# A decoder layer with a quantised feed-forward network: one more pair of blocks by two levels, and left sums built by accumulating loads

## The chip, the cores and the metric

The kernel runs on one core of one Trainium2 chip, in float32. The metric is device microseconds of one execution (us), the median of several runs. The engines are TensorE (PE, matmuls; its weight loads are listed as PEld), VectorE (DVE), ScalarE (ACT), GpSimd (POOL) and SyncE (SP, which only issues DMAs). DMAs are issued from a queue in order; those issued by SyncE and ScalarE are listed as hardware queues, those by GpSimd as a software queue. Loads that add to what their destination holds ("accumulating loads") are issued by GpSimd here.

## The reference

`x` is (16, 128, 1024), the context the same. Three residual parts follow one another; the last is most of the work:

```python
x = x + attention(layernorm(x), Wqkv, bqkv, Wo, bo)
x = x + linear_cross_attention(layernorm(x), context, ...)
x = x + ffn(layernorm(x), gate, up, down)

def dequantize(W_q, scale, zero):        # two 4-bit numbers to a byte
    w = stack([W_q >> 4 & 15, W_q & 15], -1).reshape(out, -1, 64)
    return ((w - zero[:, :, None]) * scale[:, :, None]).reshape(out, 2 * half)

g = einsum('bsh,ih->bsi', x, Wg)         # 1024 -> 2752
u = einsum('bsh,ih->bsi', x, Wu)
return einsum('bsi,hi->bsh', silu(g) * u, Wd)   # 2752 -> 1024
```

## The kernel before

The attention and the cross attention run first (until 756 us of the span). The feed-forward network is computed with Winograd's form of Strassen's scheme: a product of two 2x2 block matrices takes seven block products in place of eight, and sums of blocks on both sides and of the results.

**Gate and up.** The 2752 inner columns are cut into eleven blocks (`BLOCKS`): ten full ones of 256 columns and a remainder, `RB`. The tokens are cut into two passes (`PASSES`). A full block goes either by one level (`one_block`: seven products for gate and seven for up, matmuls of 128x512) or, two blocks at a time, by two levels (`two_levels`: seven outer products `DOWN` = 1, 2, 6, 5, 3, 7, 4, each of seven inner ones, matmuls of 128x256). A one-level block is 112 matmuls of 512 columns, a pair by two levels 196 of 256; each shows as two records in the trace's chain. In the first pass blocks 0 to 3 go by one level (block 0 beside the end of the cross attention), then the pairs in `PAIRS = [2, 3, 4]` by two levels, then `last_block` for the remainder; in the second pass all five pairs go by two levels, then the remainder. The inner left sums (`inner_left`, tiles li) are made by GpSimd, the inner right ones (ti) and the sums of the results (`got`, tiles U, V, C) by DVE; ACT copies banks (k) and applies silu. `finish` makes the products h of a quarter of a block (two halves of the tokens, two parities of the inner columns) and `store` puts them out to `h_all[blk, q, half]` in DRAM. DVE, GpSimd, ACT and SyncE follow an order written out by hand here (`InOrder`); `soon_due` and `extra` are lists of DVE steps that `multiply`'s neighbours take up one by one.

**What h is stored for.** Down takes h as the left matrix of an outer Strassen step as well: parity of the inner columns by pass. The first pass stores h as parts 1 and 2, the second as part 4 and, by `combine_h`, four combinations: 7, 5, 6 and 3. For these `load_first` loads parts 1 and 2 again (tiles hl), and DVE makes four subtractions and additions of 128x512 (tiles hc) a block and half. For the remainder `last_combinations` does the same at the start of down.

**Preparation of the weights.** `prepare` is a generator, and each `next` of it is one step. For each block and matrix it loads packed bytes (`raw`) and scales and zeros (`sz`; for down `szd`), turns them to float32 on DVE (tiles pa), makes the sums for the scheme (pc) and stores all to `wprep` in DRAM. Down's matrix ("d") takes two units a block, one for each half s; the unit with s = 1 makes one sum besides. The list `todo` is cut in three: twelve jobs in the attention (`early`), six in the cross attention (`middle`), the others in the first pass (`rest`), among which stand down's eleven blocks. `rest` is advanced by `beside` at fixed products of one-level blocks and by the last argument of `two_levels`, once an outer product.

**Down.** Seven outer steps `DOWN`, for each of which `operands` loads 20 blocks of h (tiles lq, 256 KB each, SyncE) and 10 of weights (wq), with `remainder` for the remainder's (lr, 96 rows; wr). Weights whose sum isn't stored are loaded with `load_sums`: the first term by SyncE, the next by GpSimd as an accumulating load on the same tile. `TERMS` says which: steps 5, 6 and 4 have two terms. For step 6 the sum is stored again (`kept_sums`), as step 4 uses it. Each step has seven inner products (`INNER` = 1, 5, 6, 7, 3, 4, 2), with inner sums lc and wc by DVE (`combine`), one step ahead of their use. The order of instructions in down is chosen by a scheduler. While TensorE runs step n, the loads of step n + 1 are issued. After inner product 6, DVE adds the bank to what it kept (iu, iv); then TensorE's small `extra` product for the remainder takes the same bank 6 (`po6`).

**Attention.** `early` is advanced at fixed places of the loop over four groups of tokens t: one or two steps at each f of t > 0, and (3, 3, 4, 2) steps after each `attend`. The cross attention's first load of the context (cxt) is issued after the attention.

Of the kernel before, what the change touches and what calls it, by code (L numbers as in the profile page):

```python
# [44 lines left out]
TERMS = {1: "0", 2: "2", 3: "3", 5: "01", 6: "40", 7: "4", 4: "52"}  # L45
# [13 lines left out]
class Route:  # L59


    def __init__(self, engine):
        self.engine = engine
# [17 lines left out]
def decoder_layer(  # L81
# [137 lines left out]
    def prepare(jobs, ahead, queue, vector=nc.vector, sync=nc.sync, loads_first=False):  # L219
# [4 lines left out]
        stores = deque()  # L224
        if loads_first:
            yield
# [5 lines left out]
        for k, (blk, mat, s) in enumerate(units):  # L232
# [4 lines left out]
            put()  # L237
            raw, scale, zero = loads.popleft()
            if k + ahead < len(units):
                loads.append(load_raw(*units[k + ahead], sync))  # L240
# [13 lines left out]
            if mat == "d":  # L254

                for n in range(2):
                    terms = [pair[:, n].bitcast(I32), zero[:, n]]
                    if n != s:
                        terms.reverse()
                    vector.tensor_tensor(pair[:, n], *terms, ALU.subtract)  # L260
                vector.tensor_tensor(pair, pair, scale, ALU.mult)
                if s == 0:
                    out = wprep[blk, mat] = dram.tile([6, *size], F32, name=f"wd{blk}", tag=f"wd{blk}")
                for n in range(2):
                    stores.append((wprep[blk, mat][QUARTERS.index((n, s))], pair[:, n]))
                if s == 1:
                    t = pools["c"].tile([P, 512], F32, name="pc")[: size[0]]
                    vector.tensor_tensor(t, pair[:, 0], pair[:, 1], ALU.add)
                    stores.append((wprep[blk, mat][4], t))
                yield  # L270
                continue
            pair = pair.rearrange("p n (j f) -> p (n j) f", f=P)
            vector.tensor_tensor(pair, pair.bitcast(I32), zero, ALU.subtract)
            vector.tensor_tensor(pair, pair, scale, ALU.mult)
# [15 lines left out]
            def comb(a, b, op):  # L290
                t = pools["c"].tile([P, 512], F32, name="pc")[: size[0]]
                vector.tensor_tensor(t, a, b, op)
                return t
# [17 lines left out]
    down = deque((blk, "d") for blk in range(len(BLOCKS)))  # L311
    for n in range(len(todo) - 1, MIDDLE, -1):
        todo[n:n] = [down.popleft() for _ in range(2)]
    todo += down
# [25 lines left out]
    with (  # L340
# [166 lines left out]
        for t in range(NT):  # L507
# [14 lines left out]
            for f in range(4):  # L522
# [9 lines left out]
                if t > 0:  # L532
                    for _ in range(1 + f % 2):
# [21 lines left out]
            for _ in range((3, 3, 4, 2)[t]):  # L555
                next(early, None)
# [480 lines left out]
    def operands(oq):  # L1037

        lb, wb = {}, {}
        for kc, half in ((0, 1), (0, 0), (1, 1), (1, 0)):  # L1040
            for i in range(NI):
                t = lb[kc, half, i] = pools["lq"].tile([P, TB], F32, name="lq")
                nc.sync.dma_start(t, h_all[2 * i + kc, oq, half])
# [4 lines left out]
    def load_right(oq, kc, wb):  # L1048
        for i in range(NI):
            wb[kc, i] = pools[f"wq{kc}"].tile([P, 512], F32, name="wq")  # L1050
        load_sums(oq, [(wb[kc, i], wprep[2 * i + kc, "d"]) for i in range(NI)])

    kept_sums = []

    def load_sums(oq, tiles):


        for n, term in enumerate(TERMS[oq]):
            for t, quarters in tiles:
                src = quarters[int(term)]  # L1060
                if n == 0:
                    nc.sync.dma_start(t, src)
                else:
                    nc.gpsimd.dma_start(t, src, accum_op=ALU.add)  # L1064
                    if oq == 6:
                        kept_sums.append((quarters[5], t))
# [15 lines left out]
    with ExitStack() as gs:  # L1082
# [38 lines left out]
        PAIRS = [2, 3, 4]  # L1121
# [40 lines left out]
        def combine_h(blk, half, h00, h10, h01, h11, engine, delay=2):  # L1162

            w = BLOCKS[blk][1]
            made = {}

            def comb(q, a, b, op):
                t = made[q] = chc.tile([P, TB], F32, name="hc", tag="hc")[:w]
                engine.tensor_tensor(t, a, b, op)
                store(blk, q, half, t, delay)  # L1170

            return [
                lambda: comb(7, h00, h01, ALU.subtract),
                lambda: comb(5, h01, h11, ALU.add),
                lambda: comb(6, made[5], h00, ALU.subtract),
                lambda: comb(3, h10, made[6], ALU.subtract),
            ]
# [82 lines left out]
        def last_block(ps, T, between):  # L1260


            keys = {0: (1, 2), 1: ("e", 4)}[ps]
# [7 lines left out]
            def small(half, x, u):  # L1271
# [5 lines left out]
                def mult():  # L1277
                    rows = ds(REST, REST)
                    t = ch.tile([P, TB], F32, name="h", tag="h")
                    vector.tensor_tensor(t[rows], u[rows], g[rows], ALU.mult)  # L1280
# [39 lines left out]
            def got(k, ps, add):  # L1320
# [4 lines left out]
                elif k == (1, 0):  # L1325
                    t = ch.tile([P, TB], F32, name="h", tag="h")
                    vector.tensor_tensor(t, ps, add, ALU.add)
                    vector.tensor_tensor(t, t, done[half], ALU.mult)
                    finish(half, t)
                else:  # L1330
                    t = done[half] = ct.tile([P, TB], F32, name="sg", tag="sg")
                    if add is None:
                        nc.scalar.activation(t, ps, AF.Silu)
                        vector.tensor_tensor(t, up[half], t, ALU.mult)
# [83 lines left out]
        def inner_left(L, pool, tag):  # L1418
# [9 lines left out]
            def comb(k):  # L1428
                t = L[k] = pool.tile([P, 2, CHUNKS, P], F32, name="li", tag=tag, bufs=8 if tag == "hc" else 4)
# [10 lines left out]
        def two_levels(ps, pairs, operands, between=lambda i, q: None):  # L1440
# [77 lines left out]
            def finish(i, q):  # L1518
# [5 lines left out]
                def mult(f):  # L1524
                    t = ch.tile([P, 2, HT], F32, name="h", tag="h")
                    pair = C[:, ts(f, 2)]
                    vector.tensor_tensor(t, pair[:, :, 1], pair[:, :, 0], ALU.mult)
# [3 lines left out]
                    elif s == 1:  # L1531
                        store(2 * i + f, 4, half, t)
# [3 lines left out]
            def combine(i, half, hl):  # L1536
                steps = [
                    combine_h(
                        2 * i + f,
                        half,  # L1540
                        hl[:, f, 0],
                        hl[:, f, 1],
                        hs[0, half, f],
                        hs[1, half, f],
                        vector,
                        delay=1,
                    )
                    for f in range(2)
                ]

                extra.extend(steps[f][k] for part in (0, 2) for f in range(2) for k in (part, part + 1))
# [12 lines left out]
            for n, (i, q) in enumerate(OUTERS):  # L1564
                last = n + 1 == len(OUTERS)
                if q in (1, 5):
                    sums["U" if q == 1 else "V"] = place.tile(
                        wide, F32, name="U" if q == 1 else "V"
                    )
# [19 lines left out]
                if ps == 1 and n == 0:  # L1589
                    extra.append(last_operand)  # L1590
                multiply(n, 2)
# [26 lines left out]
                between(i, q)  # L1618


                if ps == 0:
                    pass
                elif q == 3:
                    while extra:
                        extra.popleft()()
                    hl = load_first(i, 1)
                elif q == 7:
                    soon_due.append(lambda i=i, hl=hl: combine(i, 1, hl))
                elif q == 1 and i > 0 or last:
                    while soon_due:  # L1630
                        soon_due.popleft()()
                    do_extra(0, len(extra))
                    hl = load_first(i if last else i - 1, 0)
                    combine(i if last else i - 1, 0, hl)
# [4 lines left out]

        def load_first(i, half):  # L1640

            hl = xres.tile([P, 2, 2, TB], F32, name="hl", tag="X6")
            for f in range(2):
                for k in (1, 2):
                    tc.keep_in_program_order(
                        nc.sync.dma_start(hl[:, f, k - 1], h_all[2 * i + f, k, half])
                    )
            return hl
# [10 lines left out]
        def beside(n, mat, q):  # L1659
# [6 lines left out]
            if blk == 2 * PAIRS[0] - 1:  # L1666
                if n == 7:
                    route.engine = nc.sync
                    right.extend(first_operands.inner_right(DOWN[0]))
# [16 lines left out]
            elif blk == 2 * PAIRS[0] - 1:  # L1686
                steps = n in (0, 1, 2, 4, 12)
            elif blk == 1 and mat == "g":
                steps = n in (4, 5)
            else:  # L1690
                steps = n % 7 < 5 and (blk == 1 or n not in (3, 10))
# [4 lines left out]
        for blk in order:  # L1696
            if blk is None:
                two_levels(
# [3 lines left out]
                    lambda i, q: (q == 6 or i > PAIRS[0] and q not in (3, 7)) and next(rest, None),  # L1702
                )
                deep.close()
# [6 lines left out]
            if blk == 2 * PAIRS[0] - 1:  # L1711
                first_operands.pool = deep.enter_context(
                    tc.tile_pool(name="c_d", bufs=1, reuse_waits="tile")
                )
# [7 lines left out]
        chc = pool("c_hc", 8)  # L1722
# [3 lines left out]
        remaining = two_levels(1, range(NI), second_operands)  # L1726
# [16 lines left out]
    with ExitStack() as dst:  # L1743
# [7 lines left out]
        dh = pool("d_h", 4)  # L1751
# [6 lines left out]
        def last_combinations(half):  # L1758

            h = {}  # L1760
            for q in (4, "e", 1, 2):
                h[q] = dh.tile([P, TB], F32, name="dh")[:RW]
                nc.sync.dma_start(h[q], h_all[RB, q, half])
            for q, dst, a, b, op in (
                (5, 4, "e", 4, ALU.add),
                (7, "e", 1, "e", ALU.subtract),
                (6, 1, 4, 1, ALU.subtract),
                (3, 2, 2, 1, ALU.subtract),
            ):
                nc.vector.tensor_tensor(h[dst], h[a], h[b], op)  # L1770
                new_h(RB, q, half)
                nc.scalar.dma_start(h_all[RB, q, half], h[dst])

        def remainder(oq):
# [236 lines left out]
```

## Time and profile before

| | us |
|---|---|
| median of 3 runs (2205.85 to 2206.42) | 2206.3 |
| the profiled execution | 2204.94 |
| its span, first to last instruction | 2203.1 |
| TensorE busy | 2176.4 (99%) |
| DVE busy | 1522.8 (69%) |
| ACT busy | 515.7 (23%) |
| GpSimd busy | 722.3 (33%) |
| DMA, mean over the span | 210 GB/s |

TensorE's clock is granted in full throughout. The span in stages: attention to 253, cross attention to 756, block 0 beside its end, blocks 1 to 3 of the first pass from 820.65, its three pairs from 964.85, its remainder from 1224.7, the second pass's five pairs from 1262.5, its remainder from 1685.5, down from 1723.3 in seven steps of 67.4 us. Busy time is a share of engine time and says nothing of what waits for what. For that the chain of waits is read, which follows the work that ended last back to what released each step, and the idle time of TensorE with its releaser.

### The profile page before, as it was taken

Reading aid. Unit: us, or ns where it says so; the run is one execution under the profiler, and the core shown is the slowest. Engines: PE = TensorE matmul, PEld = TensorE weight load, DVE = VectorE, ACT = ScalarE, POOL = GpSimd, SP = SyncE. Lnnn points to the kernel's source line nnn. Section 1 sums busy time; section 2 is a strip of 40 time slices with the busy share of each in tenths; the row PEclk is TensorE's granted clock in tenths of the full one; section 3 lists DMA queues with packets and bytes.
Section 4 is the critical chain, followed back from the end, with each engine's and each line's share of the span. In section 5 each row is a group of like instructions: output and inputs, shape, how many; then the busy total and the mean of one; then the engine's idle time right before and its main releaser. Section 6 shows DMA issues by size and latency. Waiting matters only on the chain.

```text
span 2203.1 us, 24889 instructions
## 1 busy us (share of the span) xinstructions
PE 2176.4 (99%) x8668; PEld 1582.2 (72%) x8668; DVE 1522.8 (69%) x2077; ACT 515.7 (23%) x698; POOL 722.3 (33%) x686
## 2 busy tenths in 40 slices
PE   8999999999999999999999999999999999999998
PEld 7566555555555554468888588888887788888887
DVE  6897677888887776748788677667666635554472
ACT  2111135655665541112121112112211000000000
POOL 5453124333343364624444234444441011000100
PEclk9999999999999999999999999999999999999999
DMA  6436447768797698967777736566565988534931
GB/s 255 160 129 195 161 136 233 230 221 243 231 292 219 190 296 274 319 212 248 249 246 262 218 132 217 172 206 211 174 226 198 324 238 258 156 115 140 264 121 40
DMA packets 262102, 463.43 MB, mean 210 GB/s; under 512 B 28096, under 2 KB 121024, under 8 KB 257872
## 3 DMA queue, kind: packets, MB, share of 16 engines
q1 hardware_dynamic: 216304, 361.06, 51.0%
q0 software_dynamic: 27360, 81.55, 11.8%
q10 hardware_dynamic: 18304, 19.14, 2.8%
q8 instruction: 71, 1.16, 0.2%
q14 instruction: 63, 0.52, 0.1%
HBM read 297.14 MB, written 163.97 MB: 209 GB/s over the span
## 4 chain that ended last, share of the span: by engine, by line
PE 92%; DVE 5%; issue 1%; DMA 1%; ACT 0%; POOL 0%; SPq 0%; DVEq 0%; ACTq 0%; POOLq 0%
PE q L77 27%; PE po L1888 21%; PE p L77 10%; PE kq L77 10%; PE mm L77 8%; PE kx L77 5%; PE mm L422 4%; PE p L1210 2%; DVE pa L77 2%; PE mm L437 2%; PE mm L320 1%; DVE C L77 1%; PE tr L369 1%; DVE h L77 0%; DVE ti L77 0%
## 5 line engine op out<-in xcount | busy, mean ns | idle before, releaser
L77 PE MATMUL q<-ti,li 128*128 128x256 f32 x1344 | 308.9, 380 | 0.7 <-ACT k L77 0.6
L77 PEld LDWEIGHTS q<-ti,li 128*128 128x128 f32 x1344 | 255.5, 190 | 36.0 <-POOL li L77 1.0
L77 ACT COPY k<-q 128x512 f32<-128x512 f32 x168 | 98.3, 585 | 532.6 <-PE q L77 532.5
L852 POOL TENSOR_TENSOR qe<-qe,qrec 128x1024 f32<-128x1024 f32 x64 | 148.3, 2317 | 179.6 <-DVE qrec L77 142.2
L77 POOL TENSOR_TENSOR li<-w 128x512 f32<-128x512 f32 x112 | 154.3, 1379 | 119.5 <-PE q L77 64.4
L1888 PE MATMUL po<-wc,lc 128*128 128x256 f32 x840 | 183.4, 379 | 0.0
L1888 PEld LDWEIGHTS po<-wc,lc 128*128 128x128 f32 x840 | 159.9, 190 | 21.5
L77 POOL TENSOR_TENSOR li<-w,li 128x512 f32<-128x512 f32 x56 | 73.2, 1308 | 210.5 <-PE q L77 200.6
L77 PE MATMUL p<-b,w 128*128 128x512 f32 x304 | 133.9, 593 | 0.0
L77 DVE TENSOR_TENSOR C<-q,k 128x512 f32<-128x512 f32 x120 | 82.3, 685 | 70.8 <-PE q L77 66.8
L77 PE MATMUL kx<-ek,cxt 128*128 128x512 f32 x256 | 123.7, 606 | 4.6 <-DMA cxt<-in_cxt 4.6
L1888 PE MATMUL po<-wq,lq 128*128 128x256 f32 x560 | 126.7, 379 | 0.2 <-issue 0.2
L77 PEld LDWEIGHTS mm<-qs,m_sb 128*128 128x128 f32 x512 | 97.4, 190 | 39.7 <-issue 29.1
L77 DVE STREAM_TRANSPOSE kt<-qe 128x1024 f32<-128x1024 f32 x64 | 79.3, 1240 | 62.0 <-POOL qe L852 57.8
L77 PE MATMUL q<-b,w 128*128 128x256 f32 x512 | 121.0, 380 | 0.0
L77 PE MATMUL mm<-qs,m_sb 128*128 128x256 f32 x512 | 120.8, 380 | 0.0
L77 PE MATMUL kq<-wq_sb,xn 128*128 128x512 f32 x256 | 120.2, 593 | 0.4 <-ACT qe L840 0.4
L77 PE MATMUL kq<-wk_sb,cx 128*128 128x512 f32 x256 | 120.6, 594 | 0.0
L1888 PEld LDWEIGHTS po<-wq,lq 128*128 128x128 f32 x560 | 106.2, 190 | 15.6 <-issue 1.1
L77 DVE TENSOR_TENSOR pa<-pa,sz 128x1024 f32<-128x1024 int32 x86 | 112.7, 1311 | 2.4
L1064 POOL DMA_DIRECT2D wr<-wd x3 | 2.6, 854 | 336.7 <-DMA lq<-h 180.5
L422 PE MATMUL mm<-xnT,wqkv_sb 128*128 128x512 f32 (+1 forms) x320 | 112.5, 508 | 0.2 <-DVE xnT L77 0.2
(214 smaller groups left out, 3929.2 us busy)
## 6 DMA issues: line engine op xcount, KB each, us to landing
w<-wu SPq DMA_DIRECT2D x140, 256.0 KB, 3.4
lq<-h SPq DMA_DIRECT2D x140, 256.0 KB, 4.5
w<-wg SPq DMA_DIRECT2D x138, 256.0 KB, 2.8
kd<-kt SPq DMA_DIRECT2D x62, 512.0 KB, 3.6
qs<-kd SPq DMA_DIRECT2D x244, 128.0 KB, 3.2
ti<-r SPq DMA_DIRECT2D x22, 1024.0 KB, 7.3
h<-hc SPq DMA_DIRECT2D x80, 256.0 KB, 3.0
wq<-wd SPq DMA_DIRECT2D x70, 256.0 KB, 6.0
```

What stands on the lines that cost most here:

```text
L77: return lambda *args, **kw: self._tc.keep_in_program_order(fn(*args, **kw))
L320: tensor.matmul(ps, oT[:, d, ts(b % BPT, S)], wo_d[d][:, ts(h, 512)], start=(d == 0), stop=(d == 1),)
L369: nc.tensor.transpose(tr[:, j, :], xn[:, ts(4 * h + j, P)], ident)
L422: nc.tensor.matmul(ps[:, tokens], wqkv_sb[:, f, c, :], xnT[:, c, tokens], start=(c == 0), stop=(c == CC - 1),)
L437: nc.tensor.matmul(ps, xnT[:, c, ts(i, S)], wqkv_sb[:, 4:6, c, :], start=(c == 0), stop=(c == CC - 1),)
L852: nc.gpsimd.tensor_tensor(qe, qe, rec.unsqueeze(2).to_broadcast(wide), ALU.mult)
L1064: nc.gpsimd.dma_start(t, src, accum_op=ALU.add)
L1210: tensor.matmul(ps, wt[:, j, :], T[q][:, :, j], start=(first == q and j == 0), stop=(q in (2, 3, 4) and j == JC - 1), skip_group_check=True,)
L1888: nc.tensor.matmul(bank[:, i, :], l[:, ts(i, S)], w,  start=(start and c == 0 and i % 2 == 0), stop=(stop and c == len(pairs) - 1), skip_g ...
```

## The change

1. `PAIRS` becomes `[1, 2, 3, 4]`: blocks 2 and 3 go by two levels in the first pass.
2. Of down's weights only blocks 0 to 3 (`LATE`) are prepared in the first pass. The other seven (14 units) are prepared beside the second pass's pairs by a second generator, `downs`, whose loads have one buffer each. `two_levels` takes the generator and a function that says how many of its steps to put into `extra` at each outer product; with `fine`, a step is cut in two.
3. Each block of down's weights has its sum for step 6 stored too (t6), so that step 6 loads one term, without an accumulating load.
4. The second pass makes its products with the sign turned (`product`), stores them as parts "e" and 4, and makes one sum, part 5 (`add_up`). `combine_h`, `load_first` and `last_combinations` go.
5. In down the left operands come by `load_sums` too: `H_TERMS` says from which parts, `REST_TERMS` the same for the remainder. The second term of steps 6, 3 and 7 is an accumulating load by GpSimd, 20 blocks in each, and the remainder's have one or two (steps 6, 5, 3, 7). Step 6's left sums are stored again as part 6, which step 3 reads. Signs in down's `got` follow.
6. In the attention, two early steps are taken up sooner: at t = 2 two at each f, and none after the last `attend`.

```diff
-TERMS = {1: "0", 2: "2", 3: "3", 5: "01", 6: "40", 7: "4", 4: "52"}
+TERMS = {1: (0,), 2: (2,), 3: (3,), 5: (0, 1), 6: (5,), 7: (4,), 4: (5, 2)}
+H_TERMS = {1: (1,), 2: (2,), 6: (5, 1), 5: (5,), 3: (2, 6), 7: (1, "e"), 4: (4,)}
+REST_TERMS = {**H_TERMS, 6: ("e", 4, 1), 5: ("e", 4)}
...
+            if ahead == 0:
+                loads.append(load_raw(*units[k], sync))
+                yield
             raw, scale, zero = loads.popleft()
...
+                if fine.fine:
+                    yield
                 vector.tensor_tensor(pair, pair, scale, ALU.mult)
...
                 if s == 1:
-                    t = pools["c"].tile([P, 512], F32, name="pc")[: size[0]]
-                    vector.tensor_tensor(t, pair[:, 0], pair[:, 1], ALU.add)
-                    stores.append((wprep[blk, mat][4], t))
+                    t7, t6 = (pools["c"].tile([P, 512], F32, name="pc", tag="hc", bufs=4)[: size[0]] for _ in range(2))
+                    vector.tensor_tensor(t7, pair[:, 0], pair[:, 1], ALU.add)
+                    stores.append((out[4], t7))
+                    vector.tensor_tensor(t6, t7, A[0, 0], ALU.add)
+                    stores.append((out[5], t6))
...
-    down = deque((blk, "d") for blk in range(len(BLOCKS)))
-    for n in range(len(todo) - 1, MIDDLE, -1):
-        todo[n:n] = [down.popleft() for _ in range(2)]
-    todo += down
+    LATE = 4
+    todo += [(blk, "d") for blk in range(LATE)]
...
-                    for _ in range(1 + f % 2):
+                    for _ in range(2 if t == 2 else 1 + f % 2):
                         next(early, None)
...
-            for _ in range((3, 3, 4, 2)[t]):
+            for _ in range((3, 3, 4, 0)[t]):
...
             for i in range(NI):
-                t = lb[kc, half, i] = pools["lq"].tile([P, TB], F32, name="lq")
-                nc.sync.dma_start(t, h_all[2 * i + kc, oq, half])
+                lb[kc, half, i] = pools["lq"].tile([P, TB], F32, name="lq")
+            load_sums(
+                H_TERMS[oq],
+                [(lb[kc, half, i], h_parts(2 * i + kc, half)) for i in range(NI)],
+                oq if oq == 6 else None,
+                kept_last if (kc, half) == (1, 0) else kept_sums,
+            )
...
+    def load_sums(terms, tiles, keep=None, kept=None):
+        for n, term in enumerate(terms):
+            for t, parts in tiles:
                 if n == 0:
-                    nc.sync.dma_start(t, src)
+                    nc.sync.dma_start(t, parts[term])
                 else:
-                    nc.gpsimd.dma_start(t, src, accum_op=ALU.add)
-                    if oq == 6:
-                        kept_sums.append((quarters[5], t))
+                    nc.gpsimd.dma_start(t, parts[term], accum_op=ALU.add)
+                if keep is not None and n == len(terms) - 1:
+                    kept.append((parts[keep], t))
+
+    def keep_sums(kept):
+        while kept:
+            nc.gpsimd.dma_start(*kept.pop(0))
...
-        PAIRS = [2, 3, 4]
+        PAIRS = [1, 2, 3, 4]
...
+        def product(ps, dst, a, b):
+            if ps == 0:
+                vector.tensor_tensor(dst, a, b, ALU.mult)
+            else:
+                vector.scalar_tensor_tensor(dst, a, -1.0, b, ALU.mult, ALU.mult)
...
+                    store(2 * i + f, ("e", 4)[s], half, t)
+                    if s == 1:
+                        extra.append(lambda a=hs[0, half, f], b=t: add_up(2 * i + f, half, a, b))
...
+            def add_up(blk, half, a, b):
+                t = chc.tile([P, TB], F32, name="hc", tag="hc", bufs=4)
+                vector.tensor_tensor(t, a, b, ALU.add)
+                store(blk, 5, half, t, 1)
...
+                extra.extend([lambda: next(steps, None)] * between(n, i, q))
...
             else:
-                steps = n % 7 < 5 and (blk == 1 or n not in (3, 10))
+                steps = n in (4, 5, 8, 10, 12)
...
+                    rest,
+                    lambda n, i, q: {1: 2, 2: 1, 6: 1, 5: 2, 4: 1}.get(q, 0) if i > PAIRS[0] else q == 6,
...
+        downs = prepare([(blk, "d") for blk in range(LATE, len(BLOCKS))], 0, route, vector, route)
...
+            lambda n, i, q: {1: 2, 2: 1, 6: 2, 5: 2, 3: 1, 4: 2}.get(q, 0) if n > 2 else 0,
...
+        def load_left(oq, rem):
+            load_sums(
+                REST_TERMS[oq],
+                [(rem[0][half], h_parts(RB, half)) for half in range(2)],
+                oq if oq == 6 else None,
+                kept_last,
+            )
...
                 rem = remainder(DOWN[n + 1])
                 after = operands(DOWN[n + 1])
+                load_left(DOWN[n + 1], rem)
...
                 elif iq == 5:
                     combine(3, *now)
+                    if oq == 6:
+                        keep_sums(kept_last)
...
-                    while kept_sums:
-                        nc.gpsimd.dma_start(*kept_sums.pop(0))
+                    keep_sums(kept_sums)
```

## The prediction

> **What bounds the kernel now.** I read the chain of waits first (start, length, engine, output, line, count; all in us):
>
> ```profile
> 252.86 4.01 DMA cxt<-in_cxt
> 820.65 144.20 PE p L77 x336
> 964.85 27.64 PE q L77 x128
> 1262.50 423.03 PE q L77 x1960
> 1723.30 407.40 PE po L1888 x1886
> ```
>
> TensorE (PE) makes up nearly all of it. 144.20 us for 336 records is three one-level blocks: 48.07 a block, 0.4292 a record of 512 columns. 423.03 for 1960 records is the second pass's five pairs: 84.6 a pair, 0.2158 a record of 256 columns. The stretches by stage (us, busy time of PE, PEld, DVE, ACT and POOL, granted clock, DMA share, GB/s) show where TensorE waits, and what the other engines have left:
>
> ```profile
> 965.00:1050.00 85.00, 84.02 (x385) 72.59 (x384) 65.67 (x82) 15.84 (x25) 38.20 (x27) 1.00 0.67 232
> 1050.00:1134.00 84.00, 83.14 (x385) 73.00 (x384) 64.09 (x76) 16.70 (x26) 35.50 (x27) 1.00 0.75 251
> 1134.00:1225.00 91.00, 88.75 (x409) 77.49 (x408) 77.72 (x91) 16.70 (x26) 35.30 (x26) 1.00 0.75 245
> 1347.00:1432.00 85.00, 85.00 (x396) 74.96 (x395) 57.80 (x75) 16.95 (x27) 36.88 (x28) 1.00 0.61 200
> 1791.30:1858.70 67.40, 67.40 (x314) 59.17 (x313) 34.13 (x53) 1.45 (x2) 15.73 (x22) 1.00 0.87 258
> 1926.10:1993.50 67.40, 67.40 (x314) 59.32 (x313) 31.18 (x51) 1.01 (x1) 0.00 (x0) 1.00 0.39 126
> ```
>
> In the first pass a pair costs TensorE some 0.9 us where DVE is busy for 64 to 66 us, and 2.25 where it is busy for 77.7; the second pass (57.8) and down (the last two lines, one step each) lose nothing. So DVE, GpSimd or DMA work is free until it makes TensorE wait, and the sum is made of TensorE's own work and of waits that go or come.
>
> **The change, part by part.**
>
> *A fourth pair by two levels.* Two one-level blocks go (2 x 112 records x 0.4292 = 96.1 us), one pair comes (392 x 0.2158 = 84.6): **-11.6**. This is TensorE's own work; no cover plays a part.
>
> *Preparation in the first pass.* Four of down's blocks are prepared there instead of all eleven, but beside four pairs instead of three, and in half steps. The three pairs lost 0.98 + 0.86 + 2.25 = 4.1 us; four at 0.9 to 2.25 lose 3.6 to 9.0, so -0.5 to +4.9. Half steps shorten the unbroken stretches of DVE work that stood in front of TensorE in the third pair, so I take the low end: **0**.
>
> *Early steps of the attention.* TensorE's timeline has one stall before the feed-forward network:
>
> ```profile
> 257.00 3.75 PE L77 MATMUL kx<-ek,cxt 128*128 128x512 f32 x4 [4.64 <-DMA cxt<-in_cxt]
> ```
>
> The load is issued at 252.86, after DVE's last early step, and lands 4.0 us later. The change runs two of these steps earlier, about 8 us of DVE work in the stretch before the load, so the load can go out at least 4.6 us earlier: **-4** (0 to -4.6; some may come back, because DVE is 28 of 30 us busy where the steps go).
>
> *Second pass.* Removed: 80 combinations hc, 64.0 us in four groups, 12.8 a pair. Added: four sums a pair at some 0.8 us (3.2), and 14 preparation units of down's weights. A unit costs two raw conversions (0.49 each), two steps with szd (1.06 each), one multiplication (1.27) and on average one sum pc (0.69): 5.06, so 14.2 a pair. The products take a scalar as well; the rows of that form cost 1272 to 1842 ns for 1024 elements, 0.64 to 0.92 for the 512 of a product that now takes 1.07, so no more than now. DVE: 57.8 - 12.8 + 3.2 + 14.2 = 62.4 us a pair, near the first two pairs of the first pass, at 0.9 lost each: **+4.5** (0 to +11, five times the third pair's 2.25). The units' loads have one buffer, so DVE can also stand behind a load, with everything queued behind it; that is a rival below. The hl loads go and more stores come, with the DMA engines at 0.61; that is hidden.
>
> *Down: left sums by accumulating loads.* Before, DVE formed what steps 6, 3 and 7 read from h, under TensorE in the second pass, and SyncE loaded the results. Now GpSimd's queue adds 20 blocks of 256 KB in each of these three steps' prefetches, and the remainder's, and stores step 6's sums again. What does an accumulating load cost? DMA issues (count, KB, median us to landing):
>
> ```profile
> wq<-wd POOLq DMA_DIRECT2D x30, 256.0 KB, 8.5
> wr<-wd POOLq DMA_DIRECT2D x3, 192.0 KB, 7.1
> wd<-wq POOLq DMA_DIRECT2D x10, 256.0 KB, 3.4
> ```
>
> The first two are accumulating loads, in bursts and at the head of one; the third is a plain store of the same queue, my lower bound. GpSimd's timeline at the stores that each wait for one accumulating load:
>
> ```profile
> 1819.62 0.58 POOL L1931 DMA_DIRECT2D wd<-wq  x1 [4.69 <-DMA wq<-wd]
> 1820.89 0.56 POOL L1931 DMA_DIRECT2D wd<-wq  x1 [0.70 <-DMA wq<-wd]
> 1822.13 0.54 POOL L1931 DMA_DIRECT2D wd<-wq  x1 [0.68 <-DMA wq<-wd]
> 1823.17 0.54 POOL L1931 DMA_DIRECT2D wd<-wq  x1 [0.50 <-DMA wq<-wd]
> 1824.48 0.54 POOL L1931 DMA_DIRECT2D wd<-wq  x1 [0.77 <-DMA wq<-wd]
> ```
>
> Behind one another they land every (1824.48 - 1819.62) / 4 = 1.2 us.
>
> GpSimd's queue is in order, and in the changed kernel's instructions for step oq=2 (which prefetches 6) its DMAs alternate: additions of half 1; a store that waits for the first of them; the remainder's first addition; its second, on the same tile, which waits for the first; a store that waits for that; additions of half 0, a store, the remainder's two again, a store; and only then the five additions for (kc, half) = (1, 1). That is seven latencies T in a row until block 1 of (1, 1) has landed. DVE's queue, in order too, has the copies lc<-lq of blocks 0 and 1 of (1, 1) ahead of iu<-po, which empties the bank that TensorE's extra product needs. In the trace of before (DVE's, then TensorE's timeline):
>
> ```profile
> 1820.77 1.22 DVE L1919 TENSOR_TENSOR iu<-po,iu 128x1024 f32<-128x1024 f32 x1
> ```
>
> ```profile
> 1825.13 1.89 PE L1888 MATMUL po<-wr,lr 96*128 96x256 f32 x8
> ```
>
> Block 1 must have landed by 1825.13 less iu 1.22, wc 0.42 and lc 0.69, some 1822.6 with the passing of signals. The chain can begin when the first plain loads have landed: before, the accumulating load at 1795.96 was released so; I put it at 1798.7, about 7 us after the step's start. With T = 3.4 it ends at 1822.5 and costs nothing; with 7.1 at 1848.4, 25.8 us late; with 8.5, 35.6 late. Is T short here? Before, the step's DMA engines were 0.87 busy, 58.6 of 67.4 us; ten more accumulating loads (1.2 each) and ten more stores (0.8 each: 262 kB at the page's fastest slice, 324 GB/s) add 20, more than the step holds. So T stays near 7.1 while SyncE's 30 plain loads pass (some 24 us, four links) and then falls toward 3.4, on average 5.25 for the last three: 28.4 + 15.8 = 44.2, ending at 1842.9, **+20** (0 to +36).
>
> Steps oq=5 and oq=3 (which prefetch 3 and 7) have no stores, but block 1 of (1, 1) comes behind some 20 plain loads (0.8 each) and 12 accumulating ones (1.2 each) and a first latency of 7: 16 + 14.6 + 7 = 38 us into the step, where iu is due 31 us into it: **+6 each** (0 to +9, since these steps' engines were at 0.39 and 0.53, and the loads may overlap better). Prefetches of 5 and 4 change little: 0. Down in sum: +20 + 12 = **+32** (0 to +54).
>
> The Trainium skill, "DMA: Bandwidth & Descriptors", section "Anatomy of one DMA", gives a DMA of GpSimd's queue about 2.0 us plus its bytes at 436 GB/s, an estimate of 2.6 us here; the trace's 7.1 and 8.5 disagree, and by the page's figure the chain would be hidden and down would add nothing. Against the change speaks the same page's section "Issuing engines are not separate DMA queues": GpSimd's queue has no engines of its own, so its additions compete with SyncE's loads.
>
> **Sum.** -11.6 + 0 - 4 + 4.5 + 32 = +20.9. The profiled execution took 2204.94 us around its span of 2203.1, so it becomes 2225.8; the median of the runs is 2206.3, 1.4 more: **2227**.
>
> **Rivals.**
> - *The additions are hidden* (the other side: faster). T near 3.4 and overlapping loads in steps 5 and 3: 2206.3 - 11.6 - 4 + 4.5 = 2195, or 2190 if the second pass loses nothing as well. For it: plain stores of the same queue return in 3.4. Against it: no accumulating load's median is under 7.1. It decides as soon as down adds less than 11 us, a T of about 4.5.
> - *DVE bounds the second pass.* Each of the 14 units loads raw and szd into a single buffer; such loads take 4.5 to 4.8 us from SyncE. If half of the 14 waits reached TensorE, at 4.5 each, that is 31 instead of 4.5: 2254. For it: the first pass had a wait of 4.38 for szd in the chain. Against it: DVE has 20 us a pair to spare, and most units load a step ahead.
> - *A draw.* The chain costs half (10) and steps 5 and 3 nothing: 2206.3 - 11.1 + 10 = 2205.
> - *The fourth pair doesn't pay*, because all four lose what the third lost: +4.9 on my forecast, inside its range.
>
> **How the numbers follow.** A measurement of this kernel tells 0.2% from no change, 4.4 us: 2201.9 to 2210.7. Forecast, down adding 16 to 54 us: 0.58, slower. Hidden: 0.24, faster. Second pass: 0.10, slower. Draw: 0.08, same. So slower 0.68, same 0.08, faster 0.24. The forecast's own range is 2211 to 2249. Leaving out the faster end of the hidden case (under 2193) and the far end of the bad ones gives 2193 to 2250.
>
> **What would show it.** In the chain after, p of the one-level blocks should stand for 224 records, and cxt should be gone. The second pass's stretches should show DVE near 62 us a pair and TensorE within 1 us of full. In down, TensorE should stand idle ahead of po<-wr,lr in step oq=2 for some 20 us and in oq=5 and oq=3 for some 6 each, with DVE waiting for lq<-h on lc and GpSimd's stores waiting for lq<-h. If step oq=2 still takes 67.4 us, the forecast is wrong; if the accumulating lq<-h land in under 4.5 us, its T was.

## The result and the profile after

The changed kernel takes 2222.66 us (median of six runs, 2217.51 to 2226.48) against 2206.34 (six runs, 2205.85 to 2208.88): a ratio of 1.0071, with an interval of 1.0058 to 1.0085. It is slower by 16 us, and its runs scatter more than those of the kernel before. The profiled execution took 2220.72 us, 1.8 more than its span of 2218.9.

The chain of waits of the changed kernel shows where the stages now begin (start, length, engine, output, line, count):

```profile
814.39 48.07 PE p L79 x112
862.46 27.64 PE q L79 x128
...
1207.10 37.77 PE p L79 x88
1244.86 44.91 PE q L79 x208
...
1673.87 37.78 PE p L79 x88
```

One one-level block is left behind block 0 where there were three, the first pass's pairs run from 862.3 to 1207, the second pass's from 1244.7 to 1673.7. The block stands for 112 records, as each of the three did before (336), so a one-level block is 56 matmuls with two records each and not 112 matmuls, and the 224 records that the prediction named as a sign were a slip: two blocks of three leave 112. Its sum counted 112 records a block and isn't touched by it. From such rows, and from TensorE's first matmul of each kind, the stages are (us):

| stage | before | after | difference | forecast |
|---|---|---|---|---|
| up to block 0 | 756.1 | 749.6 | -6.5 | -4 |
| one-level blocks, then pairs, first pass | 468.4 | 457.3 | -11.1 | -11.6 + 0 |
| five pairs, second pass | 423.0 | 429.0 | +6.0 | +4.5 |
| both remainders | 75.5 | 75.5 | 0 | 0 |
| down | 472.4 | 499.5 | +27.1 | +32 |
| behind TensorE's last matmul | 7.6 | 7.9 | +0.3 | 0 |
| sum | 2203.1 | 2218.9 | +15.8 | +20.9 |

What TensorE waited for in the whole of the changed kernel (line waited for, us in total, times, longest):

```profile
PE po L1877 <- DVE iu L1908: 19.2, 3, 13.2
PE tr L379 <- ACT xn L168: 9.2, 1, 9.2
PE q L79 <- DVE ti L79: 5.7, 3, 2.8
PE q L79 <- ACT k L79: 2.7, 3, 1.3
PE po L1877 <- issue: 1.3, 1, 1.3
PE po L1877 <- DVE wc L1782: 1.1, 1, 1.1
```

The second line is the start of the kernel and was there before. The wait for cxt is gone; the first line is the new one, in down, and it is where the forecast put it: ahead of the extra product, behind iu. DVE's timeline around it shows why iu was late, and TensorE's what followed:

```profile
1823.77 0.69 DVE L1781 TENSOR_TENSOR lc<-lq 128x512 f32<-128x512 f32 x1 [22.93 <-DMA lq<-h]
1824.38 0.42 DVE L1782 TENSOR_TENSOR wc<-wq 128x256 f32<-128x256 f32 x1
1825.99 0.69 DVE L1781 TENSOR_TENSOR lc<-lq 128x512 f32<-128x512 f32 x1 [1.19 <-DMA lq<-h]
1826.60 0.42 DVE L1782 TENSOR_TENSOR wc<-wq 128x256 f32<-128x256 f32 x1
1826.93 1.22 DVE L1908 TENSOR_TENSOR iu<-po,iu 128x1024 f32<-128x1024 f32 x1
```

```profile
1828.20 3.78 PE L1877 MATMUL po<-wr,lr 96*128 96x256 f32 x8 [13.19 <-DVE iu L1908]
1903.24 3.78 PE L1877 MATMUL po<-wr,lr 96*128 96x256 f32 x8 [5.06 <-DVE iu L1908]
2108.97 1.99 PE L1877 MATMUL po<-wr,lr 96*128 96x256 f32 x8 [0.96 <-DVE iu L1908]
```

The bank that iu takes is that of inner product 6, and by 1815.0 TensorE had ended product 7 behind it as well, but DVE stood 22.9 us in its queue behind a copy of the next step's operand, whose additions had not landed. GpSimd's timeline shows the beginning of the chain and some of its links, most of them released by the landing of the link ahead:

```profile
1771.14 3.62 POOL L1087 DMA_DIRECT2D lq<-h  x4 [106.18 <-DMA lq<-h]
...
1786.93 0.87 POOL L1087 DMA_DIRECT2D lr<-h  x1 [5.28 <-DMA lr<-h]
...
1810.32 0.54 POOL L1093 DMA_DIRECT2D h<-lq  x1 [1.18 <-DMA lq<-h]
1810.85 0.89 POOL L1087 DMA_DIRECT2D lr<-h  x1
1814.95 0.81 POOL L1087 DMA_DIRECT2D lr<-h  x1 [3.21 <-DMA lr<-h]
1818.74 0.54 POOL L1093 DMA_DIRECT2D h<-lr  x1 [2.98 <-DMA lr<-h]
1819.31 4.43 POOL L1087 DMA_DIRECT2D lq<-h  x5
```

The five additions of the last line are those of (1, 1), the first thing that DVE waits for, and block 1's went out at 1819.9, 11 us after its first term had landed (1808.9). The seven extra products of down, one a step, lie 80.8, 75.0, 69.8, 67.4, 68.5 and 69.0 us apart, against 67.4 to 67.8 before. So 23 of the 27 us that down lost belong to steps oq=2 and oq=6 (prefetching 6 and 5): waits of 13.2 and 5.1 us and 2.4 of slow matmuls behind each. The rest are waits of about 1 us in oq=1, 7 and 4. Nothing was lost in oq=5 and oq=3 (prefetching 3 and 7), where the forecast had put 12 us.

### The profile page after: what moved, and what is told of

The parts are those of the page before. It is cut to its first block, busy times and chain, and to the rows that moved or that the text cites. A ratio compares the mean times of both kernels' runs of the same rounds, so it can differ in the third digit from the quotient of the medians.

```text
span 2218.9 us, 25341 instructions
## 1 busy us (share of the span) xinstructions
PE 2170.7 (98%) x8836; PEld 1614.9 (73%) x8836; DVE 1506.1 (68%) x2057; ACT 521.1 (23%) x704; POOL 766.5 (35%) x673
## 4 chain that ended last, share of the span: by engine, by line
PE 83%; DVE 7%; DMA 6%; issue 2%; POOL 1%; ACT 0%; SPq 0%; ACTq 0%; DVEq 0%; POOLq 0%
PE q L79 31%; PE po L1877 15%; PE kq L79 9%; PE mm L79 8%; PE p L79 6%; PE kx L79 5%; PE mm L432 4%; DMA wq<-wd 2%; PE mm L447 2%; PE p L1227 2%; DVE pa L79 1%; DMA x<-x_all 1%; DMA lq<-h 1%; PE mm L330 1%; DVE C L79 1%
## 5 line engine op out<-in xcount | busy, mean ns | idle before, releaser
L79 PE MATMUL q<-ti,li 128*128 128x256 f32 x1512 | 349.7, 381 | 8.5 <-DVE ti L79 5.7
L79 PEld LDWEIGHTS q<-ti,li 128*128 128x128 f32 x1512 | 287.7, 191 | 50.6 <-POOL li L79 4.6
L79 ACT COPY k<-q 128x512 f32<-128x512 f32 x189 | 110.6, 585 | 600.9 <-PE q L79 600.8
L79 POOL TENSOR_TENSOR li<-w 128x512 f32<-128x512 f32 x126 | 173.7, 1382 | 129.6 <-PE q L79 71.5
L79 POOL TENSOR_TENSOR li<-w,li 128x512 f32<-128x512 f32 x63 | 89.0, 1412 | 229.8 <-PE q L79 214.4
L79 DVE TENSOR_TENSOR C<-q,k 128x512 f32<-128x512 f32 x135 | 92.6, 686 | 70.0 <-PE q L79 67.2
L79 PE MATMUL q<-b,w 128*128 128x256 f32 x576 | 136.1, 379 | 0.0
L79 POOL TENSOR_TENSOR li<-li,w 128x512 f32<-128x512 f32 x63 | 84.0, 1334 | 122.5 <-PE q L79 122.2
L79 PEld LDWEIGHTS q<-b,w 128*128 128x128 f32 x576 | 109.4, 190 | 15.7 <-issue 1.0
L79 PE MATMUL q<-ti,w 128*128 128x256 f32 x504 | 119.1, 379 | 0.0
```

The lines of the kernel that those rows point to most:

```text
L79: return lambda *args, **kw: self._tc.keep_in_program_order(fn(*args, **kw))
```

## Experiments

The theory: in step oq=2 a chain of latencies in GpSimd's in-order queue, which a copy on DVE passes on to iu and so to TensorE. The rivals: that the DMA engines are simply too full; that the order on DVE alone is at fault; that other parts of the change cost the time.

**e2_no_additions: what do the additions cost in all?** Edit:

```diff
-H_TERMS = {1: (1,), 2: (2,), 6: (5, 1), 5: (5,), 3: (2, 6), 7: (1, "e"), 4: (4,)}
-REST_TERMS = {**H_TERMS, 6: ("e", 4, 1), 5: ("e", 4)}
+H_TERMS = {1: (1,), 2: (2,), 6: (5,), 5: (5,), 3: (2,), 7: (1,), 4: (4,)}
+REST_TERMS = {**H_TERMS, 6: ("e",), 5: ("e",)}
...
-                oq if oq == 6 else None,
+                None,
```

> Left out: the second and third terms of the left sums in down and the stores of step 6's sums, so that each left operand is one plain load. Theory: down falls from 499.5 us to the 472.4 of before, and nothing else changes: 2220.7 - 27 = 2194 for the profiled run. Rival (a part of down's loss comes from something else than the additions, such as the residual's loads or the weights' loads): down stays above 477, the run above 2199.

Measured: 2193.06 us (2191.04 to 2194.65), ratio to before 0.9935 (0.9919 to 0.9952). The steps of down are back at 67.4 to 67.7 us, and down takes 472.5. All of down's loss comes with the additions and the stores, and the rest of the change is worth 13 us.

**e1b_queue_in_order: the same DMAs in another order.** `InOrder` pins an instruction behind those written ahead of it on its engine.

```diff
-                    nc.gpsimd.dma_start(t, parts[term], accum_op=ALU.add)
+                    InOrder(tc, nc.gpsimd).dma_start(t, parts[term], accum_op=ALU.add)
...
-            nc.gpsimd.dma_start(*kept.pop(0))
+            InOrder(tc, nc.gpsimd).dma_start(*kept.pop(0))
```

> The same DMAs in down, but GpSimd's additions and stores are issued in the order in which the program writes them: all 20 additions of a step first, then the remainder's, then the stores of step 6's sums. The chain of seven latencies ahead of block 1 of (1, 1) becomes one. Theory (a chain in GpSimd's queue): TensorE's wait ahead of the extra product in step oq=2 goes from 13.2 us to 0, and with it the slow matmuls behind it (2.4 us): about 15.6 us less, some 2205 for the profiled run. The wait of 5.1 us in step oq=6 has another cause and stays. Rival (the DMA engines are simply full, whatever the order): the wait shrinks by less than 4 us, 2217 to 2221.

Measured: 2206.1 us (2202.54 to 2210.88, ten runs), ratio to before 1.0003 (0.9993 to 1.0012). The wait in step oq=2 is gone (67.5 us from extra product to extra product), as expected, and oq=6's rose from 5.1 to 8.6 us. What SyncE's queue waited for between 1830 and 1885 us, e1b:

```profile
SPq L1085 <- PE po L1877: 43.4, 7, 33.6
SPq L1085 <- DMA h<-lq: 15.4, 4, 14.7
SPq L1085 <- DMA wq<-wd: 3.1, 7, 1.3
```

The second line is new: the loads for the next step stand 14.7 us behind the stores h<-lq, which now come late and still hold the tiles lq that the loads are to fill. The order removed one wait and made another.

**e1_stores_last: half of it.** Only the second edit of e1b.

> Half of e1b: only the stores of step 6's sums are pinned behind what is written ahead of them; the additions may still be put ahead of or behind one another. In the order of GpSimd's queue there are then five latencies in a row ahead of block 1 of (1, 1) instead of seven. Theory: the wait of 13.2 us in step oq=2 falls by about two latencies, which took 3.5 to 8 us each in the changed kernel, to 0 to 6 us. Rival (any wait for a store is the whole cause): it goes to 0 in any case and the rest of the queue no longer matters, or it stays at 13.

Measured (one run, 2220.21 us): the wait in oq=2 is 8.75 us, not 0 to 6. Block 1 of (1, 1) landed 40.4 us into the step against 44.8. There are two links fewer, but some of those left are longer: additions of half 0 took 10 to 13 us from issue to landing, with more DMAs under way at once, which is the likely reason and wasn't tried. The latencies of the changed kernel went up to 11.9 us, too, and not to 8. That the wait goes neither to 0 nor stays at 13 speaks against the rival as stated; my size was wrong. The run gained nothing: down took 499.6 us, as in the changed kernel, because waits of 1.2 to 4.3 us stood in three later steps and slow matmuls followed two of them.

**e3_sums_first: leave the DMAs, change DVE's order.**

```diff
-                nc.vector.tensor_tensor(l, a, b, op)
+                (InOrder(tc, nc.vector) if k == 5 and i == 0 else nc.vector).tensor_tensor(l, a, b, op)
```

> GpSimd's queue stays as in the changed kernel up to (1, 1), but on DVE the copies lc of the next step's left operands stand behind the results of inner product 7, so that iu no longer queues behind them. Theory: the additions land as late as before (block 1 of (1, 1) some 46 us into step oq=2), yet TensorE's 13.2 us wait is gone: some 2205. The wait in oq=6 stays in part, since the copies wc, which wait for the weights, still stand ahead of iu. Rival (the late operands are needed by TensorE itself soon after): the wait comes back at the next step's product 5, and the time stays at 2217 to 2221.

Measured: 2220.33 us (2219.06 to 2221.69), ratio 1.0062 (1.0045 to 1.0078): no gain over the changed kernel. TensorE's waits, e3:

```profile
PE po L1877 <- DVE iu L1908: 13.7, 2, 10.3
...
PE po L1877 <- DVE m L1834: 3.8, 1, 3.8
```

The wait at oq=2's extra product is gone, so the copy ahead of iu was indeed how the lateness reached TensorE. But the rival was right on the time, though not on the place. DVE now stands 9 us behind the same late operands between 1819 and 1830 us. Early in oq=6 TensorE waits 3.8 us for a result m, which itself waited 4.3 us for the landing of a store of the output, and oq=6's extra product waits 10.3 in place of 5.1; one of 3.4 us follows in oq=7. Moving what stands behind the late operands only moved the wait.

**e8_no_residual: what makes oq=6 wait?** In the changed kernel's chain of waits the step reads:

```profile
1857.56 17.11 DMA x<-x_all
1874.69 5.77 DMA wq<-wd
1886.90 14.63 DMA wq<-wd
1903.24 168.09 PE po L1877 x766
```

A load of the residual x by ScalarE, 17.1 us under way, releases SyncE's load of the weights, which doesn't use x. In the program these loads wait on completion counters, a few for all DMAs of SyncE and ScalarE: in the trace the weight load waits for counter 103, which the load of x carries. The last of the three DMAs is GpSimd's addition to a weight tile. Edit: `xt = residual(oq, ib) if oq in (3, 7) else None`.

> Left out: the residual of the output quarter of step oq=2, its four loads of x and the four additions. Theory on the wait of 5.1 us in step oq=6: SyncE's loads of the weights stand 6.5 us behind the landing of one of these loads of x (17 us under way), with which they share a completion counter; without it the wait falls below 1 us and oq=2's wait of 13 us stays. Rival (the additions and stores fill the DMA engines): oq=6's wait stays at 4 us or more.

Measured (one run, 2211.11 us): oq=6's wait is gone altogether, oq=2's is 14.3 us. The first of the weight loads goes out 32.6 us ahead of the extra product, where it was 23.5 ahead of the time at which that was due. So leaving out the loads of x is enough. It doesn't show that the counter alone made the wait, since 2 MB of loads go with it, and e6, below, loses the wait with the loads of x in place.

**e6_stores_between: both ends of the conflict.** e1b, and the stores of (0, 1), (0, 0) and (1, 1) go out right behind the additions of (1, 1):

```diff
                 kept_last if (kc, half) == (1, 0) else kept_sums,
             )
+            if (kc, half) == (1, 1):
+                keep_sums(kept_sums)
```

> GpSimd's queue in down as written, but with the stores of step 6's sums between the additions of (1, 1) and those of (1, 0), so that they neither stand ahead of (1, 1) nor keep the tiles until SyncE needs them for the next loads. Theory: the wait in step oq=2 stays away (as in e1b), and oq=6's wait, 8.6 us in e1b because SyncE's loads stood 14.7 us behind the late stores, falls to 3 us or less; down 475 to 480, the run about 2196. Rival (oq=6's wait comes from the volume of DMAs, not from the stores): it stays at 5 us or more, about 2202.

Measured: 2194.75 us (2191.09 to 2195.43), ratio to before 0.9944 (0.9928 to 0.9961). Stretches of its steps oq=2 and oq=6 (us, busy time of PE, PEld, DVE, ACT, POOL, clock, DMA share, GB/s), and of the changed kernel's:

```profile
1780.50:1848.00 67.50, 67.50 (x314) 59.17 (x313) 34.20 (x53) 1.45 (x2) 23.09 (x32) 1.00 0.98 274
1848.00:1915.30 67.30, 67.30 (x313) 59.12 (x313) 32.38 (x52) 1.01 (x1) 21.12 (x27) 1.00 0.95 260
```

```profile
1781.00:1864.20 83.20, 70.01 (x314) 60.68 (x313) 33.95 (x53) 1.47 (x2) 25.98 (x36) 0.92 0.86 237
1864.20:1939.10 74.90, 69.84 (x313) 60.67 (x312) 32.30 (x52) 1.01 (x1) 17.02 (x20) 0.95 0.80 216
```

With the DMA engines at 0.98 and 274 GB/s TensorE doesn't wait at all; with 0.86 and 237 GB/s it waited 13 us. So in these steps the volume of the DMAs wasn't the limit, the order was. Down takes 472.7 us, as with no additions.

In oq=6, e6 also says more than e8. SyncE waits 6.6 us for x here, too, and its weight loads begin as late as in the changed kernel, 9.4 us behind the start of the step's first products against 9.5. What differs is GpSimd's queue. DVE's timeline ahead of iu, of the changed kernel and of e6:

```profile
1899.68 0.42 DVE L1782 TENSOR_TENSOR wc<-wq 128x256 f32<-128x256 f32 x1 [4.58 <-DMA wq<-wd]
1901.62 0.43 DVE L1782 TENSOR_TENSOR wc<-wq 128x256 f32<-128x256 f32 x1 [0.92 <-DMA wq<-wd]
```

```profile
1875.30 0.42 DVE L1784 TENSOR_TENSOR wc<-wq 128x256 f32<-128x256 f32 x1 [3.06 <-DMA wq<-wd]
1876.60 0.42 DVE L1784 TENSOR_TENSOR wc<-wq 128x256 f32<-128x256 f32 x1 [0.28 <-DMA wq<-wd]
```

The two weight tiles that iu stands behind come first and second among the additions to wq in e6, and these additions took 6.7 and 7.3 us to land. In the changed kernel they come sixth and seventh, and took 13.3 and 14.6. So two things stand behind oq=6's wait: weight loads that begin late, and an order in which the additions needed first come late. Without the one (e8) or the other (e6) the wait was gone, though both runs changed more than that.

**e4_three_pairs and e5_early: the parts that gain.** Edits: `PAIRS = [2, 3, 4]`; the two lines of the attention as before the change.

> Blocks 2 and 3 go by one level again (PAIRS = [2, 3, 4]), all else as in the changed kernel. Theory: TensorE's work grows by 11.6 us, and the first pass's pairs lose a fourth of their 6.2 us less: 2231 for the profiled run. Rival (the fourth pair doesn't pay, since preparation runs late in four pairs as well): 2221 to 2225.

> The attention's early steps as before the change, all else as in the changed kernel. Theory: TensorE waits some 4.6 us for cxt again, +4 to +6: 2225 to 2227 for the profiled run. Rival (the load of cxt is early for another reason): no change, 2221.

Measured: e4 2232.04 us (2229.68 to 2239.63), ratio 1.0124 (1.0104 to 1.0145), 9.4 above the changed kernel by the medians; the profiled spans differ by 10.4, with the first pass's blocks and pairs at 468.1 us, as before the change. The fourth pair pays nearly in full. e5 2227.28 us (2226.1 to 2229.28), ratio 1.0098 (1.0081 to 1.0115): the wait of 4.6 us for cxt is back, and block 0 begins at 755.9 us, 6.3 later.

**e7_prep_moved, e10_first_pair, e9_later_start: the waits for ti.** On top of e6:

```diff
-                    ... if i > PAIRS[0] else q == 6,
+                    ... if i > PAIRS[0] else 0,
-                steps = n in (4, 5, 8, 10, 12)
+                steps = n in (4, 5, 8, 10, 12, 13)
```

The edit above is e10. e7 has it too, with `5: 1, 3: 1, 7: 1` for `5: 2, 3: 1` in the second pass's steps; e9 is e10 with `n > 3` for `n > 2` there.

> As e6, and preparation steps moved: none in the first pass's first pair (one more in each one-level block instead), and in the second pass one step from outer product 5 to 7. Theory (TensorE's small waits for ti are DVE's preparation steps standing ahead of ti): the 2.8 us wait with its slow matmuls at the start of the first pair goes, and the second pass's 2.4 us one, together 4 to 7 us below e6. Rival (these are waits of the pairs themselves, or they come back at another outer product): within 2 us of e6.

> e6, and no preparation in the first pass's first pair, one more step in each one-level block instead (the first half of e7). Theory: the first pass's four pairs fall from 344.8 us to 340, as in e7, and the second pass stays at e6's 428.9: 4 to 5 us below e6, about 2190. Rival (the steps are late elsewhere): within 2 us of e6.

> e10, and the second pass's preparation begins one outer product later, so that none stands in the first pair's outer product 5, where TensorE waited 2.4 and 0.6 us for ti. Theory: these two waits go, the others (0.8 and 1.3) stay: 3 us below e10, about 2187. Rival (the same step makes the same wait one outer product on): the same as e10.

Measured: e7 2193.03 us (2192.14 to 2193.91), ratio 0.9939 (0.9922 to 0.9955); e10 2191.87 (2191.07 to 2192.59), 0.9932 (0.9915 to 0.9949); e9 2187.86 (2186.95 to 2188.75), 0.9913 (0.9897 to 0.9930). e7 fell short: the first pass's pairs went from 344.8 to 340.1 us, but the second pass from 428.9 to 433.2. Its wait of 2.4 us for ti stayed, so the theory missed there; the matmuls behind it now ran at half rate (1.7 us), and there are 2.8 us more of waits for k. e10 keeps the first and drops the second: 340.1, but the second pass took 430.6, so that 2.9 us were gained and not 4 to 5. Its waits are those of e6; the 1.7 us are again half rate behind the wait of 2.4 us, where e6 had full rate (see the last section). e9 removes that wait and brings the second pass to 426.6. TensorE's waits in e9:

```profile
PE tr L379 <- ACT xn L168: 9.3, 1, 9.3
PE q L79 <- ACT k L79: 3.4, 4, 1.2
PE po L1879 <- DVE wc L1784: 0.6, 1, 0.6
```

No wait for ti or iu is left. e9 beats both kernels: 0.9913 of the time before, 19 us less, with the change's own arithmetic and nothing but other orders of its DMAs and preparation steps.

## Why the prediction was right

The forecast of 2227 us and "slower" held (2222.7), and for the reason given in the main: a chain in GpSimd's queue ahead of iu in step oq=2. That down's sum came within 5 us (27.1 against 32) is partly luck: the 12 us of steps oq=5 and oq=3 didn't come, and 7.5 us in oq=6 and some 4 in oq=1, 7 and 4 came that the forecast had put at 0.

- *Fourth pair, first pass, -11.6 and 0*: -11.1 together. e4 shows it from the other side (-10.4). The four pairs lost 6.2 us against four undisturbed ones of 84.6, the three before 6.1, inside the 3.6 to 9.0 stated. That the half steps kept the loss low wasn't tried by itself.
- *Early steps, -4*: -6.5. The mechanism was right, the size was not: the forecast counted the idle time alone. The matmuls behind it ran at half rate as well: `kx` takes 3.75 us for four matmuls in the row that the prediction showed, and 1.88 in the changed kernel, another 1.9 us. So the clock of the kernel before was not in full throughout: from 254.57 to 261.40 us it stood at 0.50.
- *Second pass, +4.5*: +6.0, in four waits of 0.6 to 2.4 us for ti or k, at 63 to 66 us of DVE a pair (forecast 62.4). In the first pair TensorE stood idle for 2.9 us, more than the 1 us a pair that the prediction named as a sign. The rival of single-buffered loads, 31 us, didn't come: DVE stood 3.3 us in all behind szd. Its preparation steps stood ahead of ti (e9 moved them and gained).
- *Step oq=2, +20*: 13.2 of waiting and 2.4 of slow matmuls. The term that was mis-sized is the chain's beginning. Its first additions, of half 1, went out at 1771.14, 9.9 us ahead of the step's start at 1781.0, where the forecast had the chain begin 7.4 behind. From there block 1 took 54.7 us to land (1825.80), where 44.2 were estimated: there were eight latencies, two of them side by side, since a store of half 0 stood ahead of some of its additions. In sum it landed 44.8 us into the step in place of 51.6. Each latency was between 3.5 and 11.9 us: the longest while SyncE's loads passed, the shortest, 3.8 and 3.5, when they were nearly through, as assumed.
- *Steps oq=5 and oq=3, +6 each*: 0. This step failed. The forecast added the durations of 20 plain loads and 12 additions one behind another and set the sum against the time when iu is due; the trace shows these steps at 67.4 us and e6 the same DMA volume without a wait. Block 1 of (1, 1) landed 29.8 and 30.1 us into them, where 38 was forecast and 31 was the limit, so the wait was missed by about 1 us. Six additions of each were issued ahead of the step, from 9.7 and 7.8 us ahead on, as tiles came free; the forecast counted them as if they began with it.
- *Step oq=6, 0*: 5.1 and 2.4 of slow matmuls. Its own DMAs hardly changed, but not what they stand behind: SyncE's queue stood behind a load of x that was 17.1 us under way (e8), and the additions to the weights that were needed first came sixth and seventh (e6).
- *The argument that the additions bring 20 us more DMA work than before, more than the step holds*, was wrong as a reason: e6 fits it into 67.5 us at a share of 0.98, with part of it in the next step (0.95, where the kernel before had 0.66).

The Trainium skill, "DMA: Bandwidth & Descriptors", section "Anatomy of one DMA", gives by its fit some 2.6 us for such a DMA, an estimate. The changed kernel's additions took a median of 6.6 to 7.0 us (lq) and 7.2 (lr), so with the page's figure the forecast would have missed the wait.

## What to carry to other kernels

An in-order queue that alternates dependent and independent DMAs turns latencies into a sum: issue all that is independent first, and what waits for a landing after it, but not so late that it holds the buffers of the next loads. Price such a chain in links, each at the latency that the trace shows under load, and look for what stands behind its last link on the next engine. And when a wait moves instead of going, as in e3, look for the cause upstream of the order that was changed.

## What the runs showed of the hardware

TensorE's clock falls to half behind an idle time, and this is charged on top of the wait. Stretches of the changed kernel around and behind the wait of 13.2 us, and behind one of 2.78:

```profile
1819.30:1832.95 13.65, 4.75 (x11) 3.85 (x12) 7.99 (x15) 0.00 (x0) 7.19 (x10) 0.50 0.90 207
1828.20:1833.00 4.80, 4.80 (x11) 3.87 (x12) 4.80 (x10) 0.00 (x0) 1.08 (x2) 0.51 0.84 301
904.53:907.94 3.41, 2.99 (x7) 2.48 (x8) 1.47 (x3) 0.00 (x0) 0.00 (x0) 0.50 0.37 154
```

TensorE's timeline behind short waits, of the changed kernel (two rows), e1b and e10:

```profile
904.95 3.44 PE L79 MATMUL q<-ti,li 128*128 128x256 f32 x8 [2.78 <-DVE ti L79]
1299.02 1.97 PE L79 MATMUL q<-ti,li 128*128 128x256 f32 x8 [2.36 <-DVE ti L79]
904.43 1.97 PE L79 MATMUL q<-ti,li 128*128 128x256 f32 x8 [2.79 <-DVE ti L79]
1294.47 3.65 PE L79 MATMUL q<-ti,li 128*128 128x256 f32 x8 [2.35 <-DVE ti L79]
```

Eight such matmuls take 1.89 us undisturbed. The same wait is followed by half rate in one kernel and by full rate in another, so these runs give no limit in idle time: of the 21 waits of 2.3 to 2.9 us in the profiled executions of all kernels 10 were followed by half rate, and of the 15 of 3.4 to 14.3 us (the start of the kernel apart) all. Half rate came in stretches of 3.41 us or a multiple of it (6.83, 13.65). Those of the changed kernel begin at 904.53, 1819.30 and 1901.22 us, 268 and 24 times 3.413 us apart. That fits a clock which is set in fixed windows of this length, so that it matters where in them an idle time falls; this is inferred from the times and wasn't tried. Behind the 15 longer waits the half rate cost 2.0 to 3.5 us, and no more behind the longest: 2.4 behind 5.06 and 13.19 us, 3.5 behind 10.3 (e3). The Trainium skill, "TensorE: Matmul & The Clock Gate", section "Part 1: The HAM clock gate", has the half rate, and gives an idle window of some 3.4 us before it; the length agrees with the stretches here, but 2.35 us of idle time were enough in e10.

A second surprise: a DMA can wait for one that it has nothing to do with. What SyncE's queue waited for between 1830 and 1885 us in the changed kernel:

```profile
SPq L1085 <- DMA x<-x_all: 7.2, 2, 6.2
```

SyncE's load of weights waited 6.2 us for the landing of ScalarE's load of x, whose completion counter it shares by the trace. Without the loads of x (e8) the wait of TensorE behind it was gone; with them, and with such a wait of 6.6 us in SyncE's queue, e6 has none either. So the shared counter delays the load, and whether that costs anything depends on what comes behind it.
